# Four graph attention layers on one core: dot products of the first weights on other engines, one mask turned through DRAM, eight heads' weights in a row

## The chip, the core and the metric

The kernel runs on one NeuronCore of a Trainium2 chip. A core has five engines that run side by side, each through its own queue in a fixed order: TensorE (PE in the profile, its weight loads PEld) for matrix products, VectorE (DVE), ScalarE (ACT), GpSimd (POOL), and SyncE (SP), which issues DMA transfers here. TensorE reads its operands from SBUF, the on-chip memory of 128 partitions, and writes its sums to PSUM, another memory, which is handed out in banks. Data between DRAM and SBUF goes through 16 DMA engines.

The metric is the device time of one execution in microseconds. Each kernel is run several times, and the median counts. A profile records one execution more: every instruction with its start and length, and every packet of the DMA engines.

## The reference

There are 128 graphs of 128 nodes with 512 features, and an adjacency matrix for each. Four graph attention layers follow one another, each with a residual and a layer norm:

```python
x = _layernorm(x + _L0_gnn_ref(x, adj, ...))   # one head, features themselves
x = _layernorm(x + _L1_gnn_ref(adj, x, ...))   # W1 (512 x 1024), 4 heads; ELU; W2 (1024 x 512), 1 head
x = _layernorm(x + _L2_gnn_ref(x, adj, ...))   # 8 heads of 64 features
x = _layernorm(x + _L3_gnn_ref(x, adj, ...))   # one head, features themselves, ELU
```

A head gives every node two scores, dot products of its projected features with two vectors. The weight of an edge from i to j is `softmax(leaky_relu(s[i] + d[j]))` over the allowed edges, and the output is the weighted sum of the features. Layers 0, 2 and 3 take the softmax along the second axis of the adjacency matrix. Layer 1 takes it along the first axis (`softmax(e, axis=1)`), in both of its attention steps, so its mask is needed turned: allowed are the edges of the turned matrix and each node to itself. All is fp32.

Because a score is a dot product of `x @ W` with a vector, the kernel multiplies W with the vector once, at the start, and adds the result to W as further columns. The projection then delivers the scores as well.

## The kernel before

**Pairs and stages.** The 128 graphs are worked in 64 pairs. A pair goes through `first` (layer 0), `second` (the four heads of layer 1 and ELU), `third` (the second attention of layer 1) and `fourth` (layers 2 and 3). Between the stages lie three projections. Each is done by Strassen's scheme over two graphs and two halves (`strassen`): seven products instead of eight, with four sums of inputs made beforehand (`sums`, L869, GpSimd) and sums of outputs on VectorE and ScalarE (L892, L853, L854). The weights have seven blocks: four given, three differences made at the start by `combined` (L403). TensorE's work of the projections is L845, for `w1s`, `w2s` and `w3s`.

**Attention.** `attend` computes 128x128 scores per head: leaky ReLU on ScalarE (L769), mask and row maximum on VectorE (L782, or L777 in a quick stage), exp with its sum on ScalarE (L791). `mixed` (L916), `block` (L1011) and `heads` (L1073) are the products with the features.

**Turning.** The exp tile has to be turned before it is a weight of TensorE. `turned` does this in three steps: VectorE transposes 32x32 blocks (L739), SP writes the result to a scratch in DRAM (L742), and SP reads it back with the blocks in their new places (L746 or L751). In the plain form the result is interleaved: the tile is `[P, n // 2, P, 2]`, so the 128 columns of one head lie at every second float. `tile_of` picks one head. With `moving` the tile is in the order that a moving operand needs. In a *quick* stage TensorE does the turning with an identity (L718), and the spread of score rows over the partitions likewise (L661); elsewhere both go through DRAM. `QUICK` says which stages of the first and last pairs are quick.

**Masks.** `first` makes `m0` for layer 0 from the adjacency matrix plus the identity, and `m2` from the matrix itself, both on GpSimd (L927). TensorE turns `m2` with the identity matrix into a PSUM bank (L967), and VectorE multiplies it with `noneye`, one minus the identity, into `m1` (L970), which `second` and `third` read.

**The start.** W1 comes in 16 loads on the SP and ScalarE queues. TensorE spreads the two score vectors over all partitions in PSUM (L376). VectorE then makes 32 dot products (L476, called through `dot`): for two vectors, two heads, four blocks, two chunks. `combined` follows on VectorE. W2's dot products are already done otherwise: GpSimd multiplies (L536), ScalarE sums (L540).

**The order.** Nothing of the order on an engine is decided while the kernel runs. `plan` gives each operation a due time; `lay_out` simulates the engines with the costs that are written beside each operation (`op("PE", 0.84, ...)`) and writes out one order per engine. It also gives every buffer a place in one big SBUF arena and one of seven PSUM banks. The constants at the top of the file are its knobs: pace and shift of the pairs (`PACE`, `STRETCH`, `FIRST`, `LAST`, `SETUP`), how far an engine may look ahead (`AHEAD`, `LOADS`), and by how much the other engine must be better before a flexible copy changes sides (`EXTRA`). A change of a knob or of a cost moves instructions on all engines.

Of the kernel before, what the change touches and what calls it, by code (L numbers as in the profile page):

```python
# [23 lines left out]

STRETCH, PACE, AHEAD = 1.308, 44.0, 68.2
HOP = {"PE":0.0,"DVE":0.0,"ACT":0.7,"POOL":0.46,"SP":2.0}
SEED, SPREAD = 1, 0.0
SETUP = (-29.9,-18.0,-13.6)  # L30
QUICK = (2,0,2,2,3)
FIRST, LAST = (-64.8,-62.4,-117.1,-110.8,-116.1), ()
BANKS, PRODUCTS = 7, 2
SEES = {"PE": 0.06, "DVE": 0.06, "ACT": 0.06, "POOL": 0.06, "SP": 0.0}
TAIL = {"PE": 0.165, "DVE": 0.09, "ACT": 0.1, "POOL": 0.05, "SP": 0.0}
FLIGHT, LANDS, DESCRIBE = 1.3, 2.0, 0.00083
LANES = 8
SLACK = 2.0
EXTRA = 0.1
FLEX = ("copy",)  # L40
PIECE = 0.23
REACH = 0.0
LOADS = (46.0,10.1)


class Buf:
# [244 lines left out]
def tile_gat_stack(  # L291
# [188 lines left out]

    begin[0] = SETUP[0]
    s1 = [[spread_row(-10, r, n * 512) for n in range(2)] for r in r1]
    for n, (kh, nh) in enumerate(BLOCKS):
        def dots1(j, k, s, q=SLOT[kh, nh], nh=nh):
            for h in range(2):
                dot(
                    j, w1s[:, q, k, h * FH : (h + 1) * FH], s1[s][nh].ap[:, h * FH : (h + 1) * FH],
                    w1s[:, q, k, 2 * FH + 2 * s + h : 2 * FH + 2 * s + h + 1],
                )

        for k in range(2):
            for s in range(2):
                w1_own[kh, nh].append(mark())
                j = passing(F)
                at(2 * n + k + s / 2, "DVE", 0.75, lambda j=j, k=k, s=s, f=dots1: f(j, k, s),
                   [*w1_marks[kh, nh], s1[s][nh]], [j, w1_own[kh, nh][-1]])
    w1_ready = combined(8, w1s, w1_own, ["DVE", "DVE", "DVE", "DVE"])
    begin[0] = SETUP[1]

    b1b, b2b = lasting([P, HF], "b1t"), lasting([P, F], "b2t")  # L500
# [133 lines left out]
    def bank():  # L634
        return Buf("ps", [P, 512])
# [53 lines left out]
            rows += [(db, lambda db=db, h=h: db.ap[:, h, :]) for h in range(m)]  # L689
        return rows  # L690

    def turned(srcs, n, moving=False, ordered=False):


        m = n // len(srcs)
        zb, scr = Buf(f"zb{n}", [P, 4, n, 32]), Buf(f"scr{n}", [P, n * P])
        o = Buf(f"pt{n}", [P, 4, n, 32] if moving else [P, n // 2, P, 2])

        beside = lambda a: (lambda: o.ap[:, :, :, a].rearrange("p h i -> p h i")) if len(srcs) == 2 else (
            lambda: o.ap[:, 0].rearrange("p i k -> p k i"))  # L700
        if quick[0]:
            for a, (b, src) in enumerate(srcs):
                if ordered:
                    own = Buf("own", [P, m, P])

                    def order(own=own, src=src, copy=(nc.vector.tensor_copy, nc.scalar.copy)[a % 2]):
                        copy(
                            own.ap.rearrange("p k (r b) -> p k r b", b=4),
                            src().rearrange("p k (b r) -> p k r b", b=4),
                        )  # L710

                    op(("DVE", "ACT")[a % 2], 0.06 + 0.137 * m, order, [b], [own])
                    b, src = own, lambda own=own: own.ap
                px = bank()

                def flip(src=src, px=px):
                    for u in range(m):
                        nc.tensor.transpose(px.ap[:, u * P : (u + 1) * P], src()[:, u, :], ident)  # L718

                def taken(a=a, px=px):  # L720
                    if moving:
                        to = o.ap[:, :, a * m : (a + 1) * m, :].rearrange("p q h c -> p h q c")
                        got = px.ap[:, : m * P].rearrange("p (h q c) -> p h q c", h=m, q=4)
                    else:
                        to, got = beside(a)(), px.ap[:, : m * P].rearrange("p (h i) -> p h i", h=m)
                    (nc.vector.tensor_copy, nc.scalar.copy)[a % 2](to, got)  # L726

                op("PE", 0.12 * m, flip, [b], [px])
                op(("DVE", "ACT")[a % 2], 0.06 + 0.137 * m, taken, [px], joins=[o])
            return o  # L730
        for a, (b, src) in enumerate(srcs):
            def turn(a=a, src=src):
                if moving:
                    to = zb.ap[:, :, a * m : (a + 1) * m, :].rearrange("p b h c -> p h b c")
                elif len(srcs) == 2:
                    to = zb.ap.rearrange("p b h c -> p b (h c)").rearrange("p b (h c k) -> p h b c k", c=32, k=2)[:, :, :, :, a]
                else:
                    to = zb.ap.rearrange("p b h c -> p b (h c)").rearrange("p b (c k) -> p k b c", k=2)
                nc.vector.transpose(to, src().rearrange("p h (b c) -> p h b c", c=32))  # L739

            op("DVE", 0.075 + 0.134 * m, turn, [b], joins=[zb])
        op("SP", 0.5, lambda: nc.sync.dma_start(  # L742
            out=scr.ap, in_=zb.ap.rearrange("p b h c -> p (b h c)")
        ), [zb], [scr], dma=0.05 + 0.19 * n, desc=P)
        if moving:
            op("SP", 0.58, lambda: nc.sync.dma_start(  # L746
                out=o.ap.rearrange("p q h c -> p q (h c)"),
                in_=scr.ap.rearrange("p f -> (p f)").rearrange("(q p e) -> p q e", q=4, p=P),
            ), [scr], [o], dma=0.215 * n, desc=4 * P)
        else:  # L750
            op("SP", 0.65, lambda: nc.sync.dma_start(  # L751
                out=o.ap.rearrange("p h (q c) k -> p h q (c k)", q=4),
                in_=scr.ap.rearrange("p f -> (p f)").rearrange("(q p h e) -> p h q e", q=4, p=P, h=n // 2),
            ), [scr], [o], dma=PIECE * n, desc=2 * P * n)
        return o
# [185 lines left out]
    def first(n):  # L941
# [11 lines left out]
        for s, wv, init in ((1, w0d, 0.0), (0, w0s, b0t)):  # L953
# [5 lines left out]
                ), [x0], [jk], joins=[sc0], uses=[w0b[1 - s], b0b], port=not s)  # L959
            if s:  # L960
                rows = spread([(part(sc0, 1), 2)])
        mask(m2, at, ALU.is_le)
        pm = bank()

        def turn():
            for g in G:
                nc.tensor.transpose(pm.ap[:, g * P : (g + 1) * P], m2.ap[:, g, :], ident)  # L967
# [17 lines left out]
    def second(st, xl):  # L985
# [5 lines left out]
        for g in G:  # L991
            def col(g=g):
                return Four(xl[g].ap)

            zz.append(attend(rows[4 * g : 4 * g + 4], (xl[g], col), (m1, lambda h, g=g: m1.ap[:, g, :]), scaled=True)[0])
# [38 lines left out]
    def third(st, xl2):  # L1034

        m1, xb = st["m1"], st["xb"]
        sc2 = small("sc2", 2)
        rows = spread([(part(xl2, every, 0, F // 2), 2)])
        op("ACT", 0.2, lambda: nc.scalar.activation(
            sc2.ap, xl2.ap[:, :, 1, F // 2], AF.Identity, bias=shift2.ap[:, 0:1]  # L1040
        ), [xl2], [sc2], uses=[shift2])
        zz, ri = attend(rows, part(sc2), (m1, lambda h: m1.ap[:, h, :]))
        pt = turned([part(zz)], 2)
        x2 = [Buf("x2", [P, F]) for _ in G]
        for g in G:
            resid(x2[g], mixed(pt, g, part(xl2, g, every, slice(0, F // 2)), True), ri, g, part(xb[g]))
        norm([part(b) for b in x2])
        st["x2"] = x2
        st["xT2"] = turned([(b, lambda b=b: wide_rows(b.ap)) for b in x2], 8, ordered=True)

    def fourth(n, st, xl3):
# [10 lines left out]
        for g in G:  # L1062
            both = [attend(
                rows[8 * g + 4 * q : 8 * g + 4 * q + 4], part(xl3[g], q, slice(SH + 4, SH + 8)), (m2, lambda h, g=g: m2.ap[:, g, :])
            ) for q in range(2)]
            pt = turned([part(zz) for zz, _ in both], 8)
            for q in range(2):
                pa, ri = bank(), both[q][1]

                def heads(g=g, q=q, pt=pt, pa=pa):  # L1070
                    for u in range(4):
                        h = 4 * q + u
                        nc.tensor.matmul(  # L1073
                            pa.ap[:, u * CH : (u + 1) * CH], lhsT=tile_of(pt, h, H2),
                            rhs=xl3[g].ap[:, q, u * CH : (u + 1) * CH], start=True, stop=True,
                        )
# [143 lines left out]
```

## Time and profile before

| | |
|---|---|
| median of 3 runs | 2931.05 us (2930.61 to 2932.38) |
| the profiled execution | 2932.26 us |
| its span, first to last instruction | 2930.5 us |
| PE busy | 2875.0 us, 98% |
| PEld busy | 2400.3 us, 82% |
| DVE busy | 2608.7 us, 89% |
| ACT busy | 2365.8 us, 81% |
| POOL busy | 2214.2 us, 76% |
| DMA queue of SP and ACT | 848036 packets, 581.39 MB, 69.9% of 16 engines |
| granted TensorE clock, mean | 0.991 |

"Busy" is the time in which at least one instruction of an engine runs. TensorE's instructions are pipelined and their ends are modelled, so the distance between two starts says more than the length of one. One fp32 product appears as two MATMUL records with two LDWEIGHTS. A line such as `L967 PE MATMUL ps<-ident,arena 128*128 128x128 f32 x2` names the source line, engine, operation, output and inputs, shape and number. A wait is written as who waited for whom, the total, the number of times and the longest.

### The profile page before, as it was taken

The numbers are of one execution on the slowest core, as the hardware profiler recorded it, in microseconds if no ns is written. First come the engines' busy times: TensorE is split into PE (matmuls) and PEld (weight loads), VectorE is DVE, ScalarE is ACT, GpSimd is POOL, SyncE is SP. The second block draws the span as 40 slices with busy tenths as digits, with TensorE's granted clock in tenths as the row PEclk, the third lists the DMA queues.
The fourth block names the chain that finished last, engine by engine and source line by source line (L and its number), as shares of the span: only waits on it lengthen the run. The fifth ranks groups of instructions, "written<-read, shape, count | busy, mean of one in ns | idle before, by whom it ended". The sixth has DMA issues, their size and how long they took to land. (4 is left out here: it accounts for less than half of the span.)

```text
span 2930.5 us, 56837 instructions
## 1 busy us (share of the span) xinstructions
PE 2875.0 (98%) x14318; PEld 2400.3 (82%) x14318; DVE 2608.7 (89%) x9538; ACT 2365.8 (81%) x7949; POOL 2214.2 (76%) x2855
## 2 busy tenths in 40 slices
PE   7999999999999999999999999999999999999996
PEld 4878788888888888888888888888888888888885
DVE  7789899999999999999899999999899999999876
ACT  3567788888888888888888888888888888888777
POOL 3877778778777777777777877777877777877744
PEclk8999999999999999999999999999999999999998
DMA  4357787777777777777777777777777777777531
GB/s 123 95 165 203 203 223 212 216 222 206 219 224 205 214 220 210 218 217 216 211 221 213 220 219 213 211 216 211 215 217 222 207 213 223 206 218 220 157 96 61
DMA packets 849296, 586.33 MB, mean 200 GB/s; under 512 B 638113, under 2 KB 752033, under 8 KB 848970
## 3 DMA queue, kind: packets, MB, share of 16 engines
q1 hardware_dynamic: 848036, 581.39, 69.9%
q8 instruction: 116, 1.90, 0.3%
q14 instruction: 210, 1.72, 0.2%
q10 hardware_dynamic: 934, 1.32, 0.1%
HBM read 362.37 MB, written 220.23 MB: 199 GB/s over the span
## 5 line engine op out<-in xcount | busy, mean ns | idle before, releaser
L791 ACT ACTIVATE arena<-arena,nm 128x128 f32<-128x128 f32 x1920 | 743.6, 391 | 119.0 <-DVE nm L782 114.6
L845 PE MATMUL ps<-w2s,arena 128*128 128x257 f32 x3584 | 822.9, 380 | 4.7 <-DVE arena L1019 3.2
L845 PE MATMUL ps<-w1s,arena 128*128 128x258 f32 x3584 | 799.7, 383 | 2.8 <-DVE arena L726 1.6
L869 POOL TENSOR_TENSOR arena<-arena 128x256 f32<-128x256 f32 (+1 forms) x768 | 715.6, 948 | 103.2 <-DMA arena<-scr 59.6
L845 PEld LDWEIGHTS ps<-w1s,arena 128*128 128x128 f32 x3584 | 690.7, 193 | 125.0 <-issue 22.4
L845 PEld LDWEIGHTS ps<-w2s,arena 128*128 128x128 f32 x3584 | 678.5, 190 | 135.5 <-issue 14.8
L769 ACT ACTIVATE ps<-arena 128x128 f32<-128x128 f32 x1472 | 538.7, 369 | 48.5 <-DMA arena<-row 8.3
L782 DVE CUSTOM_DVE_ANT_0 arena<-ps,arena 128x128 f32<-128x128 f32 x1842 | 497.2, 380 | 73.9 <-ACT ps L769 71.1
L739 DVE STREAM_TRANSPOSE arena<-arena 128x512 f32<-128x512 f32 (+1 forms) x801 | 495.4, 631 | 31.0 <-POOL arena L801 23.5
L845 PE MATMUL ps<-w3s,arena 128*128 128x273 f32 x1792 | 456.6, 394 | 1.1 <-ACT arena L853 0.7
L833 ACT ACTIVATE arena<-arena,mr,rd 128x512 f32<-128x512 f32 x512 | 393.9, 805 | 25.3 <-POOL mr L829 24.0
L853 ACT COPY arena<-ps 128x258 f32<-128x258 f32 (+2 forms) x666 | 239.9, 370 | 207.1 <-PE ps L845 201.5
L845 PEld LDWEIGHTS ps<-w3s,arena 128*128 128x128 f32 x1792 | 334.0, 192 | 58.6 <-issue 3.0
L916 PE MATMUL ps<-arena 128*128 128x512 f32 x768 | 369.5, 602 | 2.0 <-DVE arena L726 1.8
L892 DVE TENSOR_TENSOR arena<-ps,arena 128x258 f32<-128x258 f32 (+2 forms) x768 | 315.0, 412 | 62.8 <-PE ps L845 60.2
L791 ACT ACTIVATION_READ_ACCUMULATOR arena<-arena,nm 128x1 f32 x1920 | 363.1, 189 | 0.0
L813 DVE BATCH_NORM_STATS2 st<-arena 128x6 f32<-128x512 f32 x512 | 335.7, 675 | 4.0 <-POOL arena L1116 2.3
L1000 POOL TENSOR_TENSOR arena<-arena,b1t 128x512 f32<-128x512 f32 x256 | 333.5, 1328 | 4.1
L927 POOL TENSOR_SCALAR arena<-arena 128x256 f32<-128x256 int32 x256 | 277.1, 1082 | 33.2 <-PE ps L845 11.5
L782 DVE DVE_READ_ACCUMULATOR2_ANT nm<- 128x1 f32 x1842 | 277.3, 151 | 0.0
L1011 PEld LDWEIGHTS ps<-arena 128*128 128x128 f32 x2048 | 248.1, 192 | 32.7 <-issue 24.8
L828 POOL TENSOR_TENSOR md<-mv,rd 128x2 f32<-128x2 f32 x256 | 51.8, 202 | 281.2 <-ACT rd L823 232.6
(99 smaller groups left out, 3852.1 us busy)
## 6 DMA issues: line engine op xcount, KB each, us to landing
scr<-arena SPq DMA_DIRECT2D x308, 512.0 KB
arena<-scr SPq DMA_DIRECT2D x308, 512.0 KB
arena<-row SPq DMA_DIRECT2D x184, 512.0 KB
arena<-in_x_dram SPq DMA_DIRECT2D x64, 512.0 KB
out_dram<-arena SPq DMA_DIRECT2D x64, 512.0 KB
arena<-row SPq DMA_DIRECT2D x185, 128.0 KB
scr<-arena SPq DMA_DIRECT2D x185, 128.0 KB
arena<-scr SPq DMA_DIRECT2D x185, 128.0 KB
```

Of the source, the lines that this page charges most:

```text
L739: nc.vector.transpose(to, src().rearrange("p h (b c) -> p h b c", c=32))
L769: nc.scalar.activation(z.ap[:, h * P : (h + 1) * P], rows[h][1](), AF.Prelu, bias=src[1]()[:, h : h + 1], alpha=SLOPE)
L782: nc.vector.tensor_tensor_reduce(out=zz.ap[:, h, :].rearrange("p (b a) -> p a b", b=4), in0=z.ap[:, h * P : (h + 1) * P].rearrange("p (a b ...
L791: nc.scalar.activation(zz.ap[:, h, :], zz.ap[:, h, :], AF.Exp, bias=nm.ap[:, h : h + 1], scale=-1.0, accum_out=rs.ap[:, h : h + 1],)
L813: op("DVE", 0.585, lambda g=g, y=y: nc.vector.bn_stats(st.ap[:, g, :], y()), [b], joins=[st])
L833: op("ACT", 0.715, lambda g=g, y=y: nc.scalar.activation(y(), y(), AF.Identity, bias=mr.ap[:, g : g + 1], scale=rd.ap[:, g : g + 1]), [b, ...
L845: nc.tensor.matmul(px.ap[:, :w], lhsT=lhs(k), rhs=rhs(k), start=(fresh and k == 0), stop=(k == nk - 1), skip_group_check=True,)
L869: op("POOL", cost, lambda: nc.gpsimd.tensor_tensor(out=own[o][1](), in0=a[1](), in1=b[1](), op=what), [a[0], b[0]], [s[o]])
L892: op("DVE", 0.075 + wide / 960, lambda: nc.vector.tensor_add(to(g, h), px.ap[:, :wide], u.ap[:, :wide]), [px, u], joins=[out[g]])
L916: op("PE", 0.885, lambda: nc.tensor.matmul(pa.ap.rearrange("p (s c) -> p s c", s=2) if paired else pa.ap, lhsT=tile_of(pt, h, 2), rhs=xv[1 ...
L927: op("POOL", 1.25, lambda: nc.gpsimd.tensor_scalar(out=m.ap, in0=a.ap, scalar1=0.0, scalar2=-BIG, op0=what, op1=ALU.mult), [a], [m])
L1000: op("POOL", 1.255, lambda g=g, c=c: nc.gpsimd.tensor_add(xl[g].ap[:, c, : 2 * FH], xl[g].ap[:, c, : 2 * FH], b1t[:, c * 2 * FH : (c + 1) ...
```

## The change

Three parts of the computation move, and the knobs of the order change with them.

1. *The first projection's dot products.* Those for the second vector (16 of 32) go to GpSimd, which multiplies two heads' columns at once, and to ScalarE, which sums each head with `accum_out`. ScalarE first copies the spread vector out of PSUM into `a1`[...]. The first of `combined`'s four subtractions for W1 goes to GpSimd.
2. *The mask.* `m2` is now the matrix mask times `noneye`, made on GpSimd, with its columns already in the order that `turned` expects. It is turned by `turned`, like an exp tile: transposes on VectorE, a write to DRAM and a read back. In quick stages `turned` uses TensorE.
3. *Eight heads.* With `apart` the turned tile of the fourth stage is `[P, n, P]`, each head's 128 columns in a row. The read from DRAM then has pieces of 32 floats where it had 64.

The knobs: `STRETCH`, `PACE`, `AHEAD`, `SETUP`, `FIRST`, `LAST`, `EXTRA`, `LOADS`; the cost of `heads` for the planner is 0.9 (`HEADS`) where it was 0.84; and `QUICK` makes the second stage quick for the last pair only, not the last two.

```diff
-STRETCH, PACE, AHEAD = 1.308, 44.0, 68.2
+STRETCH, PACE, AHEAD = 1.29, 44.82, 94.8
-SETUP = (-29.9,-18.0,-13.6)
-QUICK = (2,0,2,2,3)
-FIRST, LAST = (-64.8,-62.4,-117.1,-110.8,-116.1), ()
+SETUP = (-32.8,-21.8,-13.6)
+QUICK = (2,0,1,2,3)
+FIRST, LAST = (-64.8,-68.2,-113.2,-110.8,-116.1), (0.0,0.0,7.3,0.0,0.0)
-EXTRA = 0.1
+EXTRA = 0.2
+HEADS = 0.9
-LOADS = (46.0,10.1)
+LOADS = (52.1,10.1)
...
+    a1 = [passing(F) for _ in range(2)]
+    for n in range(2):
+        at(-9, "ACT", 0.6, lambda n=n: nc.scalar.copy(a1[n].ap, s1[1][n].ap), [s1[1][n]], [a1[n]])
...
         for k in range(2):
-            for s in range(2):
+            j = passing(F)
+            at(2 * n + k, "POOL", 1.25, lambda j=j, k=k, q=SLOT[kh, nh], nh=nh: nc.gpsimd.tensor_tensor(
+                out=j.ap, in0=w1s[:, q, k, : 2 * FH], in1=a1[nh].ap, op=ALU.mult
+            ), [*w1_marks[kh, nh], a1[nh]], [j])
+            for h in range(2):
+                w1_own[kh, nh].append(mark())
+                at(2 * n + k + h / 10, "ACT", 0.5, lambda j=j, k=k, h=h, q=SLOT[kh, nh]: nc.scalar.activation(
+                    j.ap[:, h * FH : (h + 1) * FH], j.ap[:, h * FH : (h + 1) * FH], AF.Copy,
+                    accum_out=w1s[:, q, k, 2 * FH + 2 + h : 2 * FH + 3 + h],
+                ), [j], [j, w1_own[kh, nh][-1]])
+            for s in range(1):
...
-    w1_ready = combined(8, w1s, w1_own, ["DVE", "DVE", "DVE", "DVE"])
+    w1_ready = combined(8, w1s, w1_own, ["POOL", "DVE", "DVE", "DVE"])
...
-    def turned(srcs, n, moving=False, ordered=False):
+    def turned(srcs, n, moving=False, ordered=False, apart=False):
...
-        o = Buf(f"pt{n}", [P, 4, n, 32] if moving else [P, n // 2, P, 2])
+        o = Buf(f"pt{n}", [P, 4, n, 32] if moving else [P, n, P] if apart else [P, n // 2, P, 2])
...
-                if moving:
+                if moving or apart:
                     to = zb.ap[:, :, a * m : (a + 1) * m, :].rearrange("p b h c -> p h b c")
...
+        elif apart:
+            op("SP", 0.7, lambda: nc.sync.dma_start(
+                out=o.ap.rearrange("p h (q c) -> p h q c", q=4),
+                in_=scr.ap.rearrange("p f -> (p f)").rearrange("(q p h c) -> p h q c", q=4, p=P, h=n),
+            ), [scr], [o], dma=0.415 * n, desc=4 * P * n)
...
-        mask(m2, at, ALU.is_le)
-        pm = bank()
-        def turn():
-            for g in G:
-                nc.tensor.transpose(pm.ap[:, g * P : (g + 1) * P], m2.ap[:, g, :], ident)
-        op("PE", 0.24, turn, [m2], [pm])
-        op("DVE", 0.335, lambda: nc.vector.tensor_mul(
-            m1.ap, pm.ap[:, : 2 * P].rearrange("p (g j) -> p g j", g=2), over(noneye)
-        ), [pm], [m1])
+        ma = m1
+        mask(ma, at, ALU.is_le)
+        no_self = lambda t: t.unsqueeze(1).to_broadcast([P, 2, *t.shape[1:]])
+        if quick[0]:
+            op("POOL", 0.8, lambda: nc.gpsimd.tensor_mul(m2.ap, ma.ap, no_self(noneye)), [ma], [m2])
+        else:
+            op("POOL", 0.8, lambda: nc.gpsimd.tensor_mul(
+                m2.ap.rearrange("p g (b a) -> p g a b", b=4), ma.ap.rearrange("p g (a b) -> p g a b", b=4),
+                no_self(noneye.rearrange("p (a b) -> p a b", b=4)),
+            ), [ma], [m2])
+        pm = turned([part(m2)], 2)
         zz, ri = attend(rows, part(sc0, 0), (m0, lambda h: m0.ap[:, h, :]))
+        m1 = pm, lambda g: tile_of(pm, g, 2)
...
-            pt = turned([part(zz) for zz, _ in both], 8)
+            pt = turned([part(zz) for zz, _ in both], 8, apart=True)
...
-                            pa.ap[:, u * CH : (u + 1) * CH], lhsT=tile_of(pt, h, H2),
+                            pa.ap[:, u * CH : (u + 1) * CH],
+                            lhsT=pt.ap[:, h, :],
...
-                op("PE", 0.84, heads, [pt, xl3[g]], [pa])
+                op("PE", HEADS, heads, [pt, xl3[g]], [pa])
```

More of the change, by code (lines that the diff above doesn't have):

```diff
@@ L724, in taken @@
                     else:
-                        to, got = beside(a)(), px.ap[:, : m * P].rearrange("p (h i) -> p h i", h=m)
+                        to, got = o.ap[:, a * m : (a + 1) * m, :] if apart else beside(a)(), px.ap[:, : m * P].rearrange("p (h i) -> p h i", h=m)
                     (nc.vector.tensor_copy, nc.scalar.copy)[a % 2](to, got)
@@ L993, in col @@
                 return Four(xl[g].ap)
-            zz.append(attend(rows[4 * g : 4 * g + 4], (xl[g], col), (m1, lambda h, g=g: m1.ap[:, g, :]), scaled=True)[0])
+            zz.append(attend(rows[4 * g : 4 * g + 4], (xl[g], col), (m1[0], lambda h, g=g: m1[1](g)), scaled=True)[0])
         pt = turned([part(z) for z in zz], 8, moving=True)
@@ L1041, in third @@
         ), [xl2], [sc2], uses=[shift2])
-        zz, ri = attend(rows, part(sc2), (m1, lambda h: m1.ap[:, h, :]))
+        zz, ri = attend(rows, part(sc2), m1)
         pt = turned([part(zz)], 2)
```

## The prediction

> **What bounds the kernel now.** I read the page first, then the busy times by window, then TensorE's list of waits, its timeline through one pair, and the groups by shape. The windows of 0 to 50, 50 to 100 and 1000 to 2000 us (the columns are named in the first line; the clock is a share of full speed, the DMA column the mean share of the 16 engines):
>
> ```profile
> core 0: us, PE busy (x) PEld busy (x) DVE busy (x) ACT busy (x) POOL busy (x), PEclk, DMA share, GB/s
> 0.00:50.00 50.00, 37.62 (x109) 24.19 (x110) 34.52 (x120) 10.21 (x23) 11.70 (x20) 0.90 0.45 143
> 50.00:100.00 50.00, 43.42 (x163) 31.16 (x163) 37.91 (x105) 30.53 (x92) 33.62 (x34) 0.83 0.38 108
> ...
> 1000.00:2000.00 1000.00, 1000.00 (x5010) 840.87 (x5009) 917.74 (x3386) 840.84 (x2841) 781.29 (x1013) 1.00 0.76 216
> ```
>
> In the middle TensorE is busy without a gap, at full clock. VectorE follows at 92%, DMA at 76%. TensorE's waits say the same: from 400 to 2700 us there is one, of 0.2 us. The rest lie at the two ends; the longest in the whole run:
>
> ```profile
> PE ps L575 <- ACT arena L833: 5.8, 1, 5.8
> PE ps L718 <- ACT arena L707: 5.4, 1, 5.4
> PE ps L718 <- POOL arena L801: 5.1, 2, 3.9
> PE ps L967 <- DVE arena L1019: 4.9, 2, 3.1
> ```
>
> So a microsecond taken from TensorE's own stream in every pair is worth 64 us, and one taken from another engine is worth nothing there. TensorE's timeline through a pair (start, length to the modelled end, line, count) gives the price of its parts by the distance of the starts:
>
> ```profile
> 2300.64 1.88 PE L916 MATMUL ps<-arena 128*128 128x512 f32 x4
> 2302.36 2.84 PE L1011 MATMUL ps<-arena 128*128 128x128 f32 x24
> 2305.04 2.02 PE L845 MATMUL ps<-w3s,arena 128*128 128x273 f32 x8
> ...
> 2319.35 0.38 PE L967 MATMUL ps<-ident,arena 128*128 128x128 f32 x2
> 2319.57 1.89 PE L916 MATMUL ps<-arena 128*128 128x512 f32 x4
> ...
> 2326.51 3.87 PE L1073 MATMUL ps<-arena 128*128 128x66 f32 x32
> 2330.22 1.94 PE L916 MATMUL ps<-arena 128*128 128x512 f32 x4
> ```
>
> The first projection's run of 56 starts at 2288.46 and, one pair on, at 2332.00: the period is 43.54 us.
>
> **What the Trainium skill says.** "SBUF — State Buffer", section "Door 1: The DMA port swizzle", says that SBUF is read in 16-byte lines, that full speed needs at least two hits to a line, and that a stride within the line is free. The eight heads' weights are read at every second float now, two hits to a line, so by the page their layout should cost nothing. The trace shows a small price: 32 L1073 instructions take 3.71 us, 0.116 each, though they move only 66 columns; 24 L1011 take 2.68 us, 0.112 each, with 128 columns and weights in a row; and L547, one column and weights in a row, is busy 3.6 us in 32, 0.1125 each. The columns do not set these times, so the load of the weights does, and its layout is what differs. I go by the trace, and keep "no cost" as a rival. "DMA: Bandwidth & Descriptors", section "Why small descriptors are slow (HBM only)", says that short pieces carry a fixed cost each. The trace's packet records agree: a 256-byte packet takes 19.9 ns in the mean, a 128-byte one 12.9, a 1 KB one 57. "TensorE: Matmul & The Clock Gate", section "What's actually happening", says that an idle array falls to half clock for some microseconds; the clock of 0.90 and 0.83 in the first two windows agrees.
>
> **The change, part by part.**
>
> *The mask on TensorE.* In 62 of 64 pairs (the first two stay on TensorE) the two transposes of L967 go: 2319.57 - 2319.35 = 0.22 us, 62 x 0.22 = **13.6 us less** on the bounding engine. VectorE loses L970 (0.413) and gains a 128x256 transpose (0.429): even. GpSimd gains one multiply of 128x256; L801 of that shape takes 0.811, and since the write is strided I allow up to the 1.36 of L869's 128x512. GpSimd is busy 34.0 us of a pair and goes to 34.8, behind it the norm's L828 and the sums of L869; L828 already waits 232.6 us for ScalarE, so this is covered. SP gains two issues a pair on about 29, at 0.3 to 0.6 us each. They stand in order: while the write waits for its transpose, the score rows and turned tiles behind it wait too. The mask is first needed by the second stage's scores (L782), and if it is late, L1011 is late next.
>
> *The heads' weights in a row.* 32 x 0.1117 = 3.57 for 3.71: 0.14 us a pair, x 64 = **9.0 us less**. The ends: nothing if the layout isn't the cause; no more than about 0.2 a pair (13 us), because L547 shows the same 0.112 with weights in a row. The price is paid by DMA: the read back comes in 4096 pieces of 128 bytes for 2048 of 256.
>
> *DMA.* Two such reads a pair: (4096 x 12.9 - 2048 x 19.9) / 16 = 0.76 us of the 16 engines each, 1.5 together. The mask: a write of 128 x 57 and a read of 512 x 19.9, over 16, is 1.1. From 0.76 x 43.54 = 33.1 to 35.7 us of a pair, a share of 0.83. If a 128-byte piece costs as much as a 256-byte one, 2 x 2.55 + 1.1 = 6.2 more, a share of 0.91. Hidden either way, by TensorE's 43 us; without that cover it would be its whole length.
>
> *One quick stage fewer.* The order of the instructions shows 306 single transposes and spreads with the identity before, 166 after: 124 are the masks', 16 the second stage of the last pair but one. At 0.11 each (four L718 from 2746.26 to 2746.70 take 0.44): **1.8 us less**, in a stretch (2700 to 2850) where TensorE has no gap. Its round trip through DRAM is longer, but other pairs fill it.
>
> *Copies.* The order also moves them: 258-wide copies on VectorE go from 214 to 346, 273-wide from 97 to 18, 257-wide from 47 to 62: 132 x 0.417 - 79 x 0.439 + 15 x 0.422 = +26.7 us, 0.42 a pair. VectorE then has 39.96 + 0.44 = 40.4 us in a period of 43.2, 93.6%.
>
> *The first projection's dot products.* VectorE loses 16 of 32 (two take 0.80 in its timeline, so 6.4 us) and one of four subtractions (1.23). GpSimd gains 8 products (L536's 1.237 at the same shape: 9.9 us) and that subtraction (2.36, its row on w2s), ScalarE 16 sums (L540's 0.621 + 0.190 at twice the width; I take 0.5, so 8 us) and two copies of 0.59. All of it lies in the first 40 us, where GpSimd waits 14.8 us before its first L828 and ScalarE 12.4 and 6.9. Seven products stand ahead of L828, which is the first pair's norm and on the path to the 5.4 us wait of L718: started near 12 they are done near 21, before the 23.9 at which L828 runs. If W1's last blocks land later than that, up to 4 us come on the path. Against it, the weights' differences end some 3 to 7 us earlier. By itself that buys nothing: TensorE sums W2's columns (L511) from 36.17 to 39.79, and VectorE's last subtraction ends at 39.38. The gain comes from the new order: L575, which waits 5.8 us alone at 65 us, now stands behind the second pair's 14 products. That gap, and half clock behind it, may go: I take **4 us less**, from 4 more to 12 less.
>
> Sum: 13.6 + 9.0 + 1.8 + 4 = 28.4 us. The profiled execution took 2932.26 us with a span of 2930.5; its span goes to 2902.1, and the median (1.2 us under that execution) from 2931.05 to about 2902. I put **2901**, since the heads' mean hides some short distances at the start of each run. That is 1.0% faster.
>
> **Rivals.**
>
> *Another engine or wait gives part of it back.* VectorE at 93.6%, in an order fixed beforehand, and DMA at 0.83 in bursts leave less slack for a late score or tile. For it: VectorE already works to within 2.8 us of the period. Against it: at 92% TensorE's waits in 2300 us came to 0.2. At 0.2 us a pair, 13 us are given back: 2915.
>
> *A part doesn't do what it says.* The weights' layout isn't the cause of 0.116, and the start gains nothing: 13.6 + 1.8 remain, 2915.5. For it: 4% is thin evidence, and the page on SBUF. Against it: L547 and L1011 agree at 0.112.
>
> *The start gains more.* L575's 5.8 us go, with half clock behind it, and the heads save 0.2: 2885.
>
> *Slower: the 128-byte pieces.* One mechanism: the pieces that carry the eight heads back cost more than any cover. A pair has 33.1 - 5.1 (the old reads) + 1.1 = 29.1 us of other DMA; the new reads hold 8192 pieces, 0.512 us for every ns. At 28 ns each the engines are full at 43.5 us and the gain is gone; at 30 the period is 44.5, 64 x 0.92 = 59 us more, near 2990. For it: the mean packet of this kernel takes 0.699 x 2930.5 x 16 / 848036 = 38.6 ns, and how 128-byte pieces fare into SBUF this trace doesn't show (its own run the other way). Against it: those are packets of 686 bytes in the mean, and even 256-byte ones take 19.9.
>
> **How the numbers follow.** About 0.2% is what a measurement of this kernel can tell from no change. The likeliest case 0.48 (2890 to 2912), given back 0.15, a part idle 0.12, a better start 0.12, slower 0.13. Faster by over 0.2% (under 2925): 0.48 + 0.11 + 0.12 + 0.12 = 0.83; within: 0.04, the worse end of giving back; slower: 0.13. The range reaches down to the better start and up to nearly no change, 2880 to 2930; it leaves out the slower cases and a little below.
>
> **What would show it.** No transposes against the identity by the mask's line after the first pairs; 32 heads' instructions in about 3.57 us; a period near 43.2 us; TensorE's waits in the middle still near nothing; DMA at 0.82 to 0.84; the mean 128-byte packet under 15 ns; no gap of 5 us near 65 us. The prediction is wrong if TensorE waits in the middle for the heads' tile, the mask or VectorE by over 0.3 us a pair, or if the heads still take 3.7.

## The result, and the profile after

The changed kernel takes 2945.13 us (median of 7, 2940.94 to 2949.66), the kernel before in the same comparison 2932.38 us (2930.40 to 2938.59). The ratio is 1.004, 95% interval 1.0030 to 1.0051: slower by 0.4%, where 1.0% faster was predicted. The profiled execution took 2942.33 us with a span of 2940.5, 10.0 more than before.

Busy times of the changed kernel in the three windows shown of the kernel before (columns in the first line):

```profile
core 0: us, PE busy (x) PEld busy (x) DVE busy (x) ACT busy (x) POOL busy (x), PEclk, DMA share, GB/s
0.00:50.00 50.00, 36.48 (x107) 23.56 (x108) 34.76 (x108) 19.64 (x67) 31.55 (x33) 1.00 0.46 147
50.00:100.00 50.00, 44.35 (x182) 32.43 (x180) 31.93 (x96) 33.58 (x103) 37.65 (x38) 0.91 0.33 96
1000.00:2000.00 1000.00, 993.18 (x4923) 821.49 (x4922) 912.62 (x3388) 830.08 (x2792) 777.06 (x1031) 1.00 0.85 220
```

The start looks better: the clock is 1.00 and 0.91 where it was 0.90 and 0.83. The middle is worse: TensorE has gaps, and issues 4923 instructions in 1000 us where it issued 5010; some 46 of the 87 fewer are the mask's transposes, two a pair, and the rest is time lost. VectorE is no busier than before, 913 us for 918; DMA rose from 0.76 to 0.85.

TensorE's waits, the longest sums of the whole run (who waited for whom, total us, times, longest):

```profile
PE ps L864 <- DVE arena L873: 8.2, 17, 0.8
PE ps L864 <- DVE arena L1134: 7.5, 17, 1.0
PE ps L732 <- issue: 6.0, 1, 6.0
PE ps L732 <- POOL arena L820: 5.0, 1, 5.0
```

The single long waits at the ends, which led the list before, are joined by many short ones in the middle. L864 is the projection (L845 before). L873 and L1134 are copies from PSUM on VectorE: TensorE waits until VectorE has emptied a bank. One such pair in TensorE's timeline (start, length to the modelled end, line, count, the wait ahead of it):

```profile
580.73 2.77 PE L864 MATMUL ps<-w1s,arena 128*128 128x258 f32 x12
583.88 9.94 PE L864 MATMUL ps<-w1s,arena 128*128 128x258 f32 x44 [0.37 <-DVE arena L873]
...
614.08 3.68 PE L1094 MATMUL ps<-arena 128*128 128x66 f32 x32
617.59 5.44 PE L864 MATMUL ps<-w2s,arena 128*128 128x257 f32 x24
...
624.58 2.77 PE L864 MATMUL ps<-w1s,arena 128*128 128x258 f32 x12
627.76 4.40 PE L864 MATMUL ps<-w1s,arena 128*128 128x258 f32 x19 [0.41 <-DVE arena L1134]
```

Two predicted savings are there: the heads' 32 instructions (L1094) take 617.59 - 614.08 = 3.51 us for 3.71, and no transposes of the mask stand between the products. Yet the first projection's run breaks after 12 instructions in both pairs. VectorE at the same moment:

```profile
580.86 1.49 DVE L753 STREAM_TRANSPOSE arena<-arena 128x512 f32<-128x512 f32 x2
582.27 0.20 DVE L689 STREAM_TRANSPOSE sT<-sc 128x64 f32<-128x64 f32 x1
582.39 0.34 DVE L801 CUSTOM_DVE_ANT_0 arena<-ps,arena 128x128 f32<-128x128 f32 x1
...
583.07 0.39 DVE L801 CUSTOM_DVE_ANT_0 arena<-ps,arena 128x128 f32<-128x128 f32 x1
583.30 0.16 DVE L801 DVE_READ_ACCUMULATOR2_ANT nm<- 128x1 f32 x1
583.30 0.43 DVE L873 COPY arena<-ps 128x258 f32<-128x258 f32 x1
```

It works without a pause; the copy that frees the bank stands behind transposes and four maximum instructions, and TensorE goes on only when it is done. That wait lasts 0.37 us. Shorter stalls don't appear as idle time, because the ends of the products are modelled; they show as distances between starts. Summed over all products from 400 to 2600 us, the excess over the usual distance of each shape is 44.1 us, against 4.1 before: 40 us over some 50 pairs, 0.8 a pair. 32.5 of the 44.1 lie in the run on `w1s`. The chain that ended last now goes through other engines too; the page's line of it by engine, after, and then before:

```profile
PE 49%; DVE 13%; ACT 10%; DMA 3%; issue 3%; POOL 1%; SPq 0%; ACTq 0%; DVEq 0%; POOLq 0%
```

```profile
PE 27%; DVE 1%; ACT 1%; POOL 0%; issue 0%; DMA 0%; ACTq 0%; POOLq 0%; DVEq 0%
```

Neither chain could be followed to the start: the one after reaches back to 582 us, the one before only to 2022 us, so each line's shares add up to what its chain covers. Of that, TensorE has 61% after and 89% before.

By place: the first group of heads runs 3.7 us earlier (222.94 for 226.67), first to last group takes 9.1 us more (2679.3 for 2670.2), and what follows the last group 4.6 more (38.3 for 33.7). In the middle, for pairs 10 to 55, the mean period is 43.97 us for 43.55: TensorE's own stream lost 0.22 + 0.20, and the stalls put on 0.8.

### The profile page after: what moved, and what is told of

It is laid out like the page before. It is cut to its first block, busy times and chain, and to the rows that moved or that the text cites. A ratio compares the mean times of both kernels' runs of the same rounds, so it can differ in the third digit from the quotient of the medians.

```text
span 2940.5 us, 56776 instructions
## 1 busy us (share of the span) xinstructions
PE 2874.0 (98%) x14170; PEld 2366.2 (80%) x14170; DVE 2611.5 (89%) x9576; ACT 2365.0 (80%) x7914; POOL 2238.4 (76%) x2928
## 4 chain that ended last, share of the span: by engine, by line
PE 49%; DVE 13%; ACT 10%; DMA 3%; issue 3%; POOL 1%; SPq 0%; ACTq 0%; DVEq 0%; POOLq 0%
PE ps L864 35%; PE ps L1032 5%; PE ps L935 5%; ACT ps L788 4%; ACT arena L810 3%; DVE arena L801 3%; PE ps L1094 2%; DVE arena L753 2%; DVE st L832 2%; DVE arena L941 2%; DVE arena L1101 1%; ACT arena L852 1%; DMA arena<-scr 1%; DMA scr<-arena 1%; DVE arena L911 1%
## 5 line engine op out<-in xcount | busy, mean ns | idle before, releaser
L864 PE MATMUL ps<-w1s,arena 128*128 128x258 f32 x3584 | 817.0, 384 | 23.3 <-DVE arena L873 8.0
L888 POOL TENSOR_TENSOR arena<-arena 128x256 f32<-128x256 f32 (+1 forms) x768 | 701.3, 929 | 172.9 <-DVE arena L1040 84.5
L864 PE MATMUL ps<-w2s,arena 128*128 128x257 f32 x3584 | 828.2, 382 | 4.4 <-ACT arena L554 3.3
L864 PEld LDWEIGHTS ps<-w1s,arena 128*128 128x128 f32 x3584 | 682.6, 193 | 170.6 <-issue 26.4
L864 PEld LDWEIGHTS ps<-w2s,arena 128*128 128x128 f32 x3584 | 667.7, 190 | 111.8 <-DVE arena L1040 10.0
L801 DVE CUSTOM_DVE_ANT_0 arena<-ps,arena 128x128 f32<-128x128 f32 x1850 | 510.1, 383 | 103.2 <-ACT ps L788 90.0
L753 DVE STREAM_TRANSPOSE arena<-arena 128x512 f32<-128x512 f32 (+1 forms) x865 | 520.4, 618 | 25.5 <-ACT arena L852 9.6
L864 PE MATMUL ps<-w3s,arena 128*128 128x273 f32 x1792 | 447.5, 394 | 1.1 <-DMA arena<-scr 0.8
L820 POOL TENSOR_TENSOR arena<-arena,ri 128x512 f32<-128x512 f32 (+1 forms) x192 | 170.6, 900 | 300.4 <-DVE ri L818 288.5
L864 PEld LDWEIGHTS ps<-w3s,arena 128*128 128x128 f32 x1792 | 336.3, 193 | 65.7 <-issue 6.7
L872 ACT COPY arena<-ps 128x257 f32<-128x257 f32 (+2 forms) x598 | 217.5, 374 | 201.0 <-PE ps L864 200.1
L911 DVE TENSOR_TENSOR arena<-ps,arena 128x258 f32<-128x258 f32 (+2 forms) x768 | 304.2, 413 | 29.2 <-PE ps L864 19.5
L1032 PEld LDWEIGHTS ps<-arena 128*128 128x128 f32 x2048 | 261.3, 193 | 43.2 <-issue 15.3
```

The costliest lines, as they stand in the source:

```text
L801: nc.vector.tensor_tensor_reduce(out=zz.ap[:, h, :].rearrange("p (b a) -> p a b", b=4), in0=z.ap[:, h * P : (h + 1) * P].rearrange("p (a b ...
L864: nc.tensor.matmul(px.ap[:, :w], lhsT=lhs(k), rhs=rhs(k), start=(fresh and k == 0), stop=(k == nk - 1), skip_group_check=True,)
L888: op("POOL", cost, lambda: nc.gpsimd.tensor_tensor(out=own[o][1](), in0=a[1](), in1=b[1](), op=what), [a[0], b[0]], [s[o]])
L911: op("DVE", 0.075 + wide / 960, lambda: nc.vector.tensor_add(to(g, h), px.ap[:, :wide], u.ap[:, :wide]), [px, u], joins=[out[g]])
L1032: nc.tensor.matmul(pa.ap[:, u * P : (u + 1) * P].rearrange("p (q c) -> p q c", q=4), lhsT=xl[g].ap[:, c, u * P : (u + 1) * P], rhs=pt.ap[: ...
```

## The experiments

At first two theories stood. A: VectorE, in the new order, frees PSUM banks late, and the heads' pieces are hidden. B: the heads' reads in 128-byte pieces are what TensorE waits for in the end. "Told" below means that the planner is given a cost; it moves instructions, and no data.

### The heads' tile alone, in the order of before

```diff
-            pt = turned([part(zz) for zz, _ in both], 8)
+            pt = turned([part(zz) for zz, _ in both], 8, apart=True)
...
+        elif apart:
+            op("SP", 0.65, ...  # 128-byte pieces, [P, n, P]
+            ), [scr], [o], dma=PIECE * n, desc=2 * P * n)
```

> The kernel before with the eight heads' tile in a row and nothing else; costs for the planner are as before, so that the order on every engine is the same. Theory A (VectorE's order in the changed kernel costs the time; the layout itself is a gain): the 32 heads' products take 3.51 us for 3.71, 64 x 0.20 = 12.8 us less, about 2919. Theory B (the 128-byte pieces load the DMA engines so far that tiles come late): no gain or a loss, 2930 or more.

Measured: 2998.53 us (2994.43 to 3003.14), ratio 1.0225 [1.0210, 1.0240]. Only the layout differs: every engine has the same instructions in the same order. From 1000 to 2000 us, the two longest sums among the waits of all engines in this kernel:

```profile
DVE arena L787 <- ACT ps L774: 66.0, 22, 5.2
ACT ps L774 <- DMA arena<-row: 57.2, 47, 2.7
```

and TensorE's from 400 to 2700 us:

```profile
PE ps L921 <- DVE nm L787: 32.8, 25, 2.8
```

In the kernel before, ScalarE's wait for the rows is this line of the same list:

```profile
ACT ps L769 <- DMA arena<-row: 2.3, 6, 0.6
```

So the chain is: score rows arrive late, ScalarE waits (L774), VectorE's maximum waits (L787), TensorE waits (L921), 0.6 us a pair and more in other places. The rows have the same bytes as before; what changed is the read beside them. One heads' read of 512 KB holds the DMA engines about 3.9 us here (3.5 in the changed kernel) where it held them 2.9 (medians of the first to the last packet). Theory B's time is right here, A's is wrong; but what comes late is the rows, and not first the heads' tile.

SyncE's own timeline shows where the delay arises. It issues in order; the same three issues (start, length), before and then with the tile in a row, are a heads' read (L751), the write behind it and a read of score rows (L685):

```profile
2346.99 0.64 SPq L751 DMA_DIRECT2D arena<-scr  x1
2347.72 2.09 SPq L742 DMA_DIRECT2D scr<-arena  x1
2349.91 0.37 SPq L685 DMA_DIRECT2D arena<-row  x1
```

```profile
2407.35 0.64 SPq L751 DMA_DIRECT2D arena<-scr  x1
2408.09 3.66 SPq L742 DMA_DIRECT2D scr<-arena  x1
2411.84 0.37 SPq L685 DMA_DIRECT2D arena<-row  x1
```

The issue of the read itself takes as long as before; the next issue, whatever it is, is held longer: 3.50 us for 1.87 in the median of 98 such places from 400 to 2600 us, two a pair. Once issued, a 512 KB read of rows lands after about as long as before (5.9 us for 5.8). So the rows are issued late rather than slowed behind the read in the DMA engines. Why the next issue is held was not tried apart; its length goes with the number of pieces, 2048 and 4096, near the 0.00083 us a piece that the planner has as a cost (`DESCRIBE`), 1.7 and 3.4 us.

### The changed kernel with the tile interleaved again

```diff
-        o = Buf(..., [P, n, P] if apart else [P, n // 2, P, 2])
+        o = Buf(..., [P, n // 2, P, 2])
```

(and the write, the read and `lhsT` as before; the costs told stay, so the order is that of the changed kernel)

> The changed kernel with the heads' tile interleaved again, read back in 256-byte pieces, at the same order on every engine. Theory A: the stalls of TensorE at the first projection stay, the heads take 3.71 us again: 2945 to 2958. Theory B: DMA falls from 0.85 to 0.79, the stalls (0.8 us a pair) go: 2945 - 51 + 13, about 2907.

Measured: 2944.59 us (2941.98 to 2946.70), ratio 1.0040 [1.0025, 1.0055]. The DMA share falls from 0.85 to 0.77, and the time stays where it was. TensorE's stalls from 400 to 2600 us are 36.4 us for 44.1, and its heads take 3.71 us again for 3.51. So in this order the slower reads cost something, about what the heads give back, and B does not explain the changed kernel's loss.

### The changed kernel with less work on VectorE

```diff
-nc.vector.bn_stats(st.ap[:, g, :], y())
+nc.vector.bn_stats(st.ap[:, g, :], y()[:, : F // 2])
```

This leaves out half of the layer norm's statistics; the order stays.

> The changed kernel with the norms' statistics over the first half of the features, at the same order on every engine; this leaves out half of the statistics. It takes some 2 us a pair from VectorE. Theory A: TensorE no longer waits for VectorE, the period falls from 43.93 to about 43.15, the time to 2890 to 2905. Theory B: nothing changes within 5 us.

Measured: 2909.26 us (2908.72 to 2911.67), ratio 0.9922 [0.9907, 0.9937], 36 us below the changed kernel. TensorE's waits from 400 to 2700 us:

```profile
PE ps L1032 <- DMA arena<-scr: 2.6, 4, 1.4
PE ps L1032 <- DVE ri L818: 1.1, 1, 1.1
PE ps L864 <- DMA arena<-scr: 1.0, 1, 1.0
```

These are the three longest; the waits for L873 and L1134 are gone, the median period is 43.12 us (43.54 less the 0.42 of both savings), and the stalls fall from 44.1 to 16.2 us, with the slower reads still in it (DMA 0.86). So most of what TensorE loses in the changed kernel, 28 of the 40 us, goes through VectorE.

### All three parts with the knobs of before

```diff
-STRETCH, PACE, AHEAD = 1.29, 44.82, 94.8
+STRETCH, PACE, AHEAD = 1.308, 44.0, 68.2
```

(and the other knobs likewise, `QUICK` among them; `HEADS` 0.9; `SLACK` 1.5 for 2.0, since the arena doesn't hold the buffers otherwise, here and in the next two)

> All three parts of the change with the planner's knobs of the kernel before (STRETCH, PACE, AHEAD, SETUP, FIRST, LAST, EXTRA, LOADS, QUICK); the slack between two uses of SBUF is 1.5 for 2.0, so that it fits. Theory A (an order that the new knobs made): another order loses less, 2895 to 2925. Theory B (DMA): the loss stays, 2935 or more.

Measured: 2955.08 us (2952.18 to 2957.87), ratio 1.0073 [1.0056, 1.0090]. The new knobs (and `SLACK`) are worth 10 us to the three parts.

### The mask alone, and the dot products alone, with the knobs of before

```diff
-                nc.tensor.transpose(pm.ap[:, g * P : (g + 1) * P], m2.ap[:, g, :], ident)
+        pm = turned([part(m2)], 2)
```

> The kernel before with the mask turned through DRAM alone, the old knobs, and a slack of 1.5 for 2.0 between two uses of SBUF, so that it fits. Theory A (VectorE, in an order laid out anew): TensorE's stream is 0.22 us a pair shorter, the waits for VectorE decide, 2915 to 2950. Theory D: DMA gains only 2%, so it comes to 2915 to 2922.

Measured: 2920.92 us (2917.84 to 2923.60), ratio 0.9961 [0.9947, 0.9975]. This beats both kernels. Its middle:

```profile
1000.00:2000.00 1000.00, 998.78 (x4975) 838.34 (x4974) 948.68 (x3460) 828.54 (x2783) 794.09 (x1036) 1.00 0.79 222
```

VectorE is busy 94.9%, the most of all these kernels, and TensorE has hardly a gap; the stalls are 7.2 us, the mean period 43.40. The mask's saving reaches the end, and a high share on VectorE is not by itself a wait. Its wait in the changed kernel comes from where instructions stand.

```diff
-            for s in range(2):
+            for s in range(1):
...
```

(the other vector's products go to GpSimd and ScalarE, and one subtraction to GpSimd, as in the change)

> The kernel before with the first projection's dot products moved alone, the old knobs, and a slack of 1.5 for 2.0. All theories: nothing changes in the middle; the start gains 0 to 6 us, 2925 to 2933. If it is slower by more than 5, the first pair's norm waits behind GpSimd's products.

Measured: 2940.20 us (2937.41 to 2945.65), ratio 1.0026 [1.0018, 1.0033]. The period is 43.54 as before; the first group of heads runs at 234.09 for 226.67. TensorE's longest wait in this kernel, and one further down the list:

```profile
PE ps L731 <- POOL arena L940: 6.0, 1, 6.0
...
PE ps L858 <- ACT arena L553: 3.5, 3, 1.8
```

The first of these is not the loss: the kernel before has the same wait, 5.4 us put down to ScalarE, and there it ends at 26.98 us, here at 27.05. The first projection then starts at 31.82 us for 29.80, so 2 us are lost by there; the other 5 come in before the first group of heads. The second line is one of the waits on that way that the kernel before doesn't have: TensorE waits for ScalarE's sums of W2's dot products, and ScalarE now has W1's to do as well. The part loses its 8 us at the start; how they divide among the engines was not settled.

### The new knobs alone

```diff
-STRETCH, PACE, AHEAD = 1.308, 44.0, 68.2
+STRETCH, PACE, AHEAD = 1.29, 44.82, 94.8
```

(and the rest of the knobs of after, on the kernel before; `SLACK` 1.0)

> The kernel before, none of the three parts, with the new knobs (QUICK among them) and a slack of 1.0 for 2.0. If the new knobs make the bad order: TensorE waits for VectorE at the first projection as in the changed kernel, 2940 or more. If the parts make it: 2925 to 2937.

Measured: 2996.24 us (2994.66 to 2998.48), ratio 1.0214 [1.0199, 1.0229], with no operation changed. Stalls of 61.6 us, half of them on `w1s`. An order that suits the three parts can cost 64 us without them.

### The heads alone, told

```diff
-            ), [scr], [o], dma=PIECE * n, desc=2 * P * n)   # 128-byte pieces
+            ), [scr], [o], dma=0.415 * n, desc=4 * P * n)
```

(and `heads` at 0.9 for 0.84; knobs of before). Here theory C says that an order made for the slower read repairs the loss, D that nothing in the order does.

> The heads' tile in a row, the knobs of the kernel before, and the planner told what the change tells it: a read of 0.415 a head for 0.23, twice the descriptors, 0.9 for the heads. The order is a new one. Theory C (the loss of 66 us with the old order is a question of what stands behind the slower reads, and a plan that knows of them avoids it): below 2950, and the ScalarE waits for rows from DMA go from 57 us in the middle 1000 us to under 10. Theory D (the reads themselves cost it, whatever the order): 2980 or more.

Measured: 2965.23 us (2961.11 to 2970.90), ratio 1.0109 [1.0094, 1.0124]: half of the 66 us comes back, between C and D. The waits for rows are gone; TensorE now loses 25.5 of its 40.3 us of stalls at the step from L1016 to the third projection.

> The order of heads_told (its costs and knobs, so the same instructions in the same order on every engine), but the eight heads' tile interleaved again, so that its read back has 256-byte pieces. heads_told gave 2965, 33 us over the kernel before. If the slow reads lose the 33 us (slow-read theory): 2930 to 2945. If the order made for the slow reads loses them (order theory): 2960 to 2978, since TensorE also gets back its 9 us. Something between says both.

The same order, with the tile interleaved: 2956.96 us (2956.13 to 2964.49), ratio 1.0088 [1.0071, 1.0105]. It falls just under the range that the order theory had given. With the quicker reads, and 12.8 us more on TensorE for the heads, it is still 24 us over the kernel before. Most of the 33 us are the order's; the slower reads cost 8 us more than the heads give back.

### The changed kernel less its heads' part

```diff
-            pt = turned([part(zz) for zz, _ in both], 8, apart=True)
+            pt = turned([part(zz) for zz, _ in both], 8)
-HEADS = 0.9
+HEADS = 0.84
```

With the knobs of before, and with the new ones (`SLACK` 1.5 in both):

> The dot products' and the mask's part, without the heads' part, with the knobs of before (SLACK 1.5). If the parts add up, 2921 (mask alone) plus 8 (dot products alone) = 2929, between 2924 and 2934, and the 22 us that the three parts together lost with these knobs are the heads' part. If the heads' part is not what loses them: 2950 or more.

> The changed kernel without the heads' part (tile interleaved, its planned costs those of before), with the knobs of after (SLACK 1.5). If the heads' part is what costs the changed kernel its gain: 2915 to 2930. If the new knobs make an order that lets TensorE wait for VectorE whatever the parts (they lost 64 us on the kernel before alone): 2945 or more, with the first projection's products waiting for PSUM banks by over 0.5 us a pair.

Measured: 2924.02 us (2921.89 to 2926.92), ratio 0.9968 [0.9955, 0.9981], and 2927.77 us (2923.24 to 2931.35), ratio 0.9984 [0.9976, 0.9991]. Against the same knobs with the heads' part, 2955.08 and 2945.13, that part costs 31 and 17 us. Without it the kernel is faster than before with either set of knobs. The dot products cost 3 us here and not 8, beside the mask; the two intervals (with and without them) overlap, so these 3 us are not clear of noise.

### One quick stage fewer

```diff
-QUICK = (2,0,2,2,3)
+QUICK = (2,0,1,2,3)
```

(on the kernel with the mask alone)

> mask_only (2921) with the second stage quick for the last pair only, as in the changed kernel. The 16 single products with the identity that this takes off TensorE are worth 1.8 us if TensorE's stream sets the end there: 2919, between 2917 and 2921. If the longer way through DRAM comes late at the end: 2923 to 2930.

Measured: 2925.88 us (2923.35 to 2928.97), ratio 0.9974 [0.9964, 0.9985], 5 us over the mask alone. Its interval and that of the mask alone overlap, so these 5 us stand at the edge of noise. From the last group of heads to the end it is 39.0 us for 32.7 in the profiled executions. Of these 6.3 us, 2.9 are the group itself: its 32 instructions take 6.7 us at a granted clock of 0.50, where they took 3.8 at 1.00. That the longer way through DRAM comes late there, where no other pairs fill it, fits, but no wait in the trace shows it.

### The slower reads in an order that was not told, and the told costs apart

Three kernels from the one with 2927.77: the tile in a row with nothing told; then the tile interleaved with one cost told at a time. As control, the changed kernel with `SLACK` 1.5.

```diff
 layout_untold:  [P, n, P], 128-byte pieces;  dma=PIECE * n, desc=2 * P * n
 told_desc:      interleaved;                 dma=PIECE * n, desc=4 * P * n
 told_dma:       interleaved;                 dma=0.415 * n, desc=2 * P * n
 after_slack:    the changed kernel, SLACK = 1.5
```

> The order of mask_dots_new (2927.8), with the eight heads' tile in a row, so the read back in 128-byte pieces, and the planner not told. If only the told costs lose time: 2916 to 2922 (2927.8 less the heads' 9). If the slower reads lose it wherever the order was made without them (as in heads_only, +66): 2950 or more, with ScalarE waiting in the middle for score rows that a DMA brings.

> mask_dots_new with one cost changed for the planner: the heads' read back is told to have twice as many descriptors (4 x 128 x 8), so SP's issue and the read look longer; the layout stays interleaved. If this cost makes the bad order: 2940 to 2950. If not: 2922 to 2934.

> mask_dots_new with one cost changed for the planner: the heads' read back is told to hold the DMA engines 3.3 us (0.415 x 8) for 1.8; the layout stays interleaved. If this cost makes the bad order: 2940 to 2950. If not: 2922 to 2934.

> The changed kernel with SLACK 1.5 for 2.0, the value that mask_dots_new has. If the told costs lose the 17 us: 2938 to 2952. If SLACK had a share: between 2925 and 2936.

Measured: `layout_untold` 2998.75 us (2991.65 to 3007.53), ratio 1.0231 [1.0208, 1.0253]; `told_desc` 2940.52 (2937.98 to 2942.11), 1.0030 [1.0018, 1.0042]; `told_dma` 2938.58 (2930.72 to 2940.95), 1.0021 [1.0014, 1.0027]; `after_slack` 2940.89 (2937.40 to 2943.36), 1.0035 [1.0022, 1.0047].

ScalarE's wait for the rows from 1000 to 2000 us, first in the kernel with the mask and the dot products under the new knobs, then in the same order with the tile in a row:

```profile
ACT ps L788 <- DMA arena<-row: 19.2, 19, 2.1
```

```profile
ACT ps L788 <- DMA arena<-row: 48.4, 30, 4.4
```

The layout alone costs 71 us in this order and cost 66 in the other: in both orders made without the slower read, score rows come late. SyncE's issue behind a heads' read takes 2.80 us here for 1.69. In the orders made with it (the changed kernel's and that of the heads alone, told) no wait of ScalarE for rows is left from 1000 to 2000 us, and the layout costs about as much as it gives, or 8 us more; but these orders let TensorE wait longer at the first projection or before the third. Either of two told costs makes 11 to 13 us of that loss, on the interleaved tile, with the stalls in the same place (17.1 us and 20.0 us on `w1s`, where the kernel with 2927.77 has 9.3). The profiled execution of `told_dma` was its shortest, 2930.72 us, so its trace shows less than its median. They don't add up: with both, and the tile in a row, `after_slack` is at +13. Of the 17 us, 4 lie between the two values of `SLACK`, but the ranges overlap, and by the ratios it is 1.5; this is not clear of noise. Why that order puts VectorE's copies later, and whether other costs would give one that doesn't, was not settled.

## Why the prediction was wrong, point by point

The parts, from the kernel before to the changed one (each difference of two medians): mask -11.5, dot products +3.1 beside it, knobs with one quick stage fewer +3.7, heads' part +17.4. They make +12.7, as they must, being steps of one way; the +3.1 and the +3.7 are not clear of noise, and on another way they would be others.

- **The mask, -13.6 predicted.** Right: -11.5 alone, the median period 0.23 lower (43.31 for 43.54). Two more issues on SP and more turning on VectorE were hidden, as said.
- **The heads' weights, -9.0 predicted.** The mechanism was right and larger than said: 3.51 us for 3.71, 12.8 us in 64 pairs, at the bound that the prediction gave. "SBUF — State Buffer", section "Door 1: The DMA port swizzle", calls a stride within the line free; for these weights the trace shows 0.118 us an instruction at every second float and 0.112 in a row (the median distance of two starts), also where nothing else changes, and the measurement decides. But none of it reached the end.
- **The failed step: "Hidden either way, by TensorE's 43 us".** The packets cost what lay within the bounds: 16.5 ns for 128 bytes, 19.0 for 256, where 12.9 was taken, and a DMA share of 0.85 for 0.83, far from full. "DMA: Bandwidth & Descriptors", section "Why small descriptors are slow (HBM only)", and these numbers agree that half the bytes are not half the time. The error was to ask only whether 16 engines have room in 43 us. A read has a length of its own, 3.5 to 3.9 us for 2.9, and SyncE's next issue is held behind it, 3.50 us for 1.87, twice a pair, so the score rows after it are issued late. The prediction priced SyncE's two new issues for the mask (on "about 29" a pair; the trace has 31), and for the heads' reads it put SyncE's time at nothing. The runs put +66 and +71 us on that when the order isn't made for it, and +17 and +31 us on the heads' part with an order that is, under the new and the old knobs. The rival of the 128-byte pieces named the right part but the wrong point: it wanted full engines, at 28 ns a piece; the loss came at 16.5 ns and 0.83.
- **What the changed kernel does instead.** Its order is made for the slower read, and gives most of the time away at VectorE: stalls of 0.8 us a pair in all, 0.6 with the quicker reads put back, where "0.2 us a pair are given back" was the rival. The prediction moved instructions in its sums (26.7 us more copies on VectorE) but judged the result by the share, 93.6% against 92%. The share was 91.3%, lower than forecast, and TensorE waited; in the mask's kernel it was 94.9%, and TensorE didn't. The sign that was written down for being wrong, TensorE waiting for VectorE by over 0.3 us a pair in the middle, is what came by the distances between starts; the list of waits alone holds 0.28.
- **One quick stage fewer, -1.8 predicted.** It did not come: +5 on the mask's kernel, at the edge of noise, and 4.6 us more at the end of the changed one, 1.8 of them in the last group of heads at a granted clock of 0.62 for 1.00. "Other pairs fill it" is the likely fault, as the last pairs have few behind them; that is argued, not shown.
- **The start, -4 predicted.** Right for the changed kernel by its first group of heads, 3.7 us earlier, and the gap of L575 near 65 us is gone. By itself the part gains nothing: it loses 8 us with the old knobs. With the mask beside it the first group runs at 228.5 under the old knobs and at 219.2 under the new ones; the new knobs alone, without any part, put it at 224.0, and the mask alone, under the old ones, too. So the gain takes the new knobs together with the parts; what the dot products give under the new knobs was not run apart.

## What to carry to other kernels

In a schedule fixed beforehand, cost a slower transfer by what stands behind it on the engine that issues it, not by the mean share of the DMA engines. Cost a busy engine by the burst ahead of the instruction that frees a buffer, not by its share: with VectorE at 94.9% TensorE hardly waited, and at 91.3% it lost 0.8 us a pair. When a part's cost is told to a planner, compare it with a kernel that has the new order and the old operation, since the order alone can be worth more than the operation.

## What the runs showed of the hardware

In the changed kernel the mean packet of 256 bytes takes 19.0 ns and that of 128 bytes 16.5, so halving the pieces made one 512 KB read grow from 2.9 to between 3.5 and 3.9 us; the median packet of 128 bytes is still 13 ns, and long ones raise the mean. The issue that SyncE makes next after such a read was held 3.50 us for 4096 pieces and 1.87 for 2048, while the read's own issue took 0.63 us in both. And of TensorE's 44 us of stalls in the middle less than half appear in its list of waits (18 us); the rest is seen only in the distance between the starts of its products.
